# The second product of a feed-forward layer computed with seven half-size products instead of eight

## The chip, the cores and the metric

The kernel runs on one core of a Trainium2 chip. The metric is the device time in microseconds, the median of several runs. All data is fp32 unless a line says otherwise. Engines are called PE (TensorE), DVE (VectorE), ACT (ScalarE), POOL (GpSimd) and SP (SyncE, which issues nearly all DMAs).

## The reference, cut to what matters

The input has four batches of 2048 tokens of 256 features. It is normalized, and two branches run on the normalized `xn`: a linear-attention layer with its feed-forward part, and a gated feed-forward with 4-bit block quantization. Their product is added to the input.

```python
def _L0_attn_ref(src, Wq, bq, ...):
    q = (src @ Wq + bq).reshape(b, s, H, DH)      # k, v alike; H = 16, DH = 64
    Q = elu(q) + 1.0
    K = elu(k) + 1.0
    KV = einsum('bshd,bshm->bhdm', K, v)
    Z = 1.0 / (einsum('bshd,bhd->bsh', Q, K.sum(axis=1)) + EPS)
    o = einsum('bshd,bhdm,bsh->bshm', Q, KV, Z).reshape(b, s, H * DH)
    x = layer_norm(src + o @ Wo + bo, g1, be1)
    y = gelu(x @ W1 + b1) @ W2 + b2               # W1 256 x 1024, W2 1024 x 256
    return layer_norm(x + y, g2, be2)

def _L0_ffn_ref(x, w_gate, w_up, w_down):
    h = silu(fp4_linear(x, w_gate)) * fp4_linear(x, w_up)
    return fp4_linear(h, w_down)                  # quantized in blocks of 16

xn = layernorm(x)
s = _L0_attn_ref(xn, ...)
g = silu(_L0_ffn_ref(xn, ...))
out = x + s * g
```

The change concerns one product, `gelu(...) @ W2`.

## The kernel before

The 8192 tokens are worked in 32 blocks of 256 tokens (`NBLK` = 32, eight blocks a batch, `NB` = 8). A block is two tiles of 128 tokens, because a tile has 128 partitions. Attention needs the key sums of a whole batch before its first query, so blocks 0 to 23 also carry the keys of the batch after theirs (`keys_k`, `keys_xk`, two tiles, "subs", a block), and blocks 24 to 31 have no key work. The keys of batch 0 are made in a prologue, during which the weights are loaded one after the other (`later`, L182 to L193; a tiny POOL copy in `load_when` holds each load back until some `kk` is there).

The main loop (L967 to L1074) issues, for block n, in this order on PE:

1. `q_of(n)`: the query product `pq`, its exponential on ACT, `zq` on DVE;
2. the keys of the first sub: product `pk`; on DVE the add of the bias `k1` (L471); the exponential `ek` on ACT; the combination `kk` on DVE (L480); the product `pxk` of `kk` with `xn_k`;
3. `sums(n)` (L747): `pz`, on DVE `z = 1/pz`, which goes to memory and comes back spread over the partitions as `zb` (four DMAs);
4. `gate_up(n+1)` and `down(n)`: the quantized branch, products `pg` and `pd`. After `pd`, ACT makes `g` and three POOL operations of 128x512 (L713 to L715) follow as a burst;
5. `qz(n)` (L774): two DVE multiplications of 128x1024, `zq *= zb`;
6. the keys of the second sub (`pk`, `k1`, `kk` as in 2);
7. `attention(n)` (L780): 16 matmuls `pa` of `zq` with the folded matrix `m`; on DVE the sum `x1 = xn + pa` and its normalization;
8. `pxk` of the second sub;
9. `ffn_2(n-1)`: the product `py` = `hT` x `w2_sb` for the block before, split: 12 of its 16 matmuls here (in blocks without keys four stand before `attention` and eight here);
10. `x1_T(n)`: transposes `pt_x` of x1, then `spread_scales(n+1)`: a transpose `pscale` of the quantization scales, which go to memory and come back spread in eight DMAs as `qT`, which `pd` of the next block reads; between and after them the last four matmuls of `py`;
11. `output(n-1)` (L842): on DVE `s = x1 + py`, the statistics, two scalings, and the store;
12. `ffn_1(n)` (L811): the product `pf`, and on ACT the GELU that writes `hT`, the transposed hidden layer (8 chunks of 128 hidden features by 256 tokens).

An fp32 `mm` of the code is two MATMUL instructions on PE. PE's order is exactly that of the program:

```python
    def mm(*args, **kw):
        return tc.keep_in_program_order(nc.tensor.matmul(*args, **kw))
```

The other engines keep program order in the prologue only. In the main loop a scheduler at build time sets the order of the operations of DVE, ACT, POOL and SP, unless `tc.issue_after(x)` puts an operation behind x. All DVE and ACT operations are recorded by a helper at L115, so the profile names that line for all of them.

Buffers: `ps` has four PSUM banks that rotate under the tag "mm" (`mm_tile`), `pacc` has two "acc" banks for `pa` and `py` (`acc_tile`) and two for `pxk`. In SBUF a tag is a set of slots that tiles take in turn: `zb` has one slot, `s` one, `kv` one, `ksum` one, `x1` two, `kk` three, `big` (with `hT`) two. A tile that takes a slot waits for the last reader of the tile before it.

The second product before, for token tile j:

```python
    def ffn_2(n, j, chunks=range(NF)):
        ...
        for c in chunks:
            mm(
                py[:, j, :], hT[:, c, j * P : (j + 1) * P], w2_sb[:, c, :],
                start=c == 0, stop=c == NF - 1,
            )
```

With NF = 8 chunks and two tiles that is 16 matmuls of N=256, 32 instructions.

Of the kernel before, what the change touches and what calls it, by code (L numbers as in the profile page):

```python
# [8 lines left out]
F32 = mybir.dt.float32  # L9
# [3 lines left out]
ALU = mybir.AluOpType  # L13
AX = mybir.AxisListType

P = 128
# [6 lines left out]
def linear_attention_gated_by_fp4_ffn(  # L23
# [34 lines left out]
    nc = tc.nc  # L58
    B, S, D = src.shape
# [6 lines left out]
    NF = FF // P  # L66
# [21 lines left out]
    def acc_tile(name, tag="acc"):  # L88
        return pacc.tile([P, 512], F32, tag=tag, name=name)

    def rows_of(dst, n):

        b, bi = divmod(n, NB)
        return dst[b, bi * T : (bi + 1) * T, :].rearrange("(p j) d -> p j d", j=TB)
# [34 lines left out]
    def load_when(dep, t, v, eng=nc.sync):  # L129

        if dep is not None:
            first = t[:1, 0, :1] if len(t.shape) == 3 else t[:1, :1]
            nc.gpsimd.tensor_copy(first, dep[:1, :1])
        eng.dma_start(t, v)
# [30 lines left out]

    wq_sb = const.tile([P, ND, HD], F32, name="wq_sb")
    w1_sb = const.tile([P, ND, FF], F32, name="w1_sb")
    w2_sb = const.tile([P, NF, D], F32, name="w2_sb")
    row_tiles = {
        name: const.tile([P, 1, D], F32, name=f"{name}_r")  # L170
        for name in ("bo", "g1", "shift", "g2", "be2")
# [3 lines left out]
    def by_chunks(w):  # L175
        return w.rearrange("(c p) f -> p c f", p=P)

    def load_row(name, v, dep):
        load_when(dep, row_tiles[name][:, 0, :], as_rows(v))


    later = {  # L182
        0: [lambda dep: load_row("bo", bo, dep)],
# [5 lines left out]
            lambda dep: load_row("g2", g2, dep),  # L189
            lambda dep: load_row("be2", be2, dep),  # L190
        ],
        5: [lambda dep: load_when(dep, w2_sb, by_chunks(W2))],
    }  # L193

    cols = {}
# [265 lines left out]
    def key_product(xnT, f, j, nm):  # L461

        fs = slice(f * HALF, (f + 1) * HALF)
        pk = mm_tile(f"pk_{nm}_{j}")
        for c in range(ND):
            mm(
                pk, xnT[:, c, j * P : (j + 1) * P], wk_sb[:, c, fs],
                start=c == 0, stop=c == ND - 1,
            )
        k1 = work.tile([P, HALF], F32, tag="q1", name=f"k1_{nm}_{j}", bufs=3)  # L470
        vector.tensor_tensor(k1, pk, bk1[:, fs], ALU.add)  # L471
        e = work.tile([P, HALF], F32, tag="e", name=f"ek_{nm}_{j}", bufs=3)
        keys["exp"] = scalar.activation(e, k1, AF.Exp, bias=neg_one).ins
        return k1, e
# [40 lines left out]
    def m_of_half(b, f, dep=None, ahead=False):  # L515


        nm = f"{b}_{f}"
        fs = slice(f * HALF, (f + 1) * HALF)
        wv = batch.tile([P, ND, HALF], F32, tag="wv", name=f"wv_{nm}", bufs=1)  # L520
        load_when(dep, wv, by_chunks(Wv)[:, :, fs])
        wo = batch.tile([P, 4, D], F32, tag="wo", name=f"wo_{nm}", bufs=1)
        load_when(dep, wo, by_chunks(Wo)[:, 4 * f : 4 * f + 4, :])
        if ahead:
            yield
        if f == 0:
            kh[b] = batch.tile([P, NH, 32], F32, tag="kh", name=f"kh_{b}")
            nc.gpsimd.memset(kh[b], 0.0)
        m = m_sb[b, f] = batch.tile([P, 4, D], F32, tag="m", name=f"m_{nm}", bufs=3)
        kacc = keys.pop((b, "acc", f))  # L530
        pxk = keys.pop((b, "pxk", f))
        xk = batch.tile([P, ND, HALF], F32, tag="xk", name=f"xk_{nm}", bufs=1)
        for d in range(ND):
            scalar.copy(xk[:, d, :], pxk[d])

        pks = mm_tile(f"pks_{nm}")
        mm(pks[:1, :], ones[:, 0:1], kacc, start=True, stop=True)
        krow = work.tile([P, HALF], F32, tag="x1T", name=f"krow_{nm}", bufs=1)[:1, :]
        scalar.copy(krow, pks[:1, :])
        k_d = dram.tile([1, HALF], F32, tag="k_d", name=f"k_d_{nm}", bufs=2)  # L540
        nc.sync.dma_start(k_d, krow)
        yield
        ksum = work.tile([P, 4, P], F32, tag="ksum", name=f"ksum_{nm}", bufs=1)
        nc.sync.dma_start(
            ksum, k_d.rearrange("o (c f) -> o c f", c=4).to_broadcast([P, 4, P])
        )

        own = work.tile([P, 4, P], F32, tag="kv", name=f"own_{nm}", bufs=1)
        kcol = small.tile([P, 4], F32, tag="kcol", name=f"kcol_{nm}")
        vector.tensor_tensor(own, ksum, ident.unsqueeze(1).to_broadcast([P, 4, P]), ALU.mult)  # L550
        vector.tensor_reduce(kcol, own, AX.X, ALU.add)
        for i in range(2):
            hs = slice(i * DH, (i + 1) * DH)
            r0 = 2 * f + i
            vector.tensor_copy(kh[b][hs, 4 * f : 4 * f + 4, r0], kcol[hs, :])
        yield

        pkv = mm_tile(f"pkv_{nm}")[:, : 4 * DH].rearrange("p (c f) -> p c f", c=4)
        kv = work.tile([P, 4, P], F32, tag="kv", name=f"kv_{nm}", bufs=1)
        nc.gpsimd.memset(kv, 0.0)  # L560
        for ci in range(4):
            for d in range(ND):
                for h in range(2):
                    cs = slice(ci * P + h * DH, ci * P + (h + 1) * DH)
                    mm(
                        pkv[h * DH : (h + 1) * DH, ci, :], wv[:, d, cs], xk[:, d, cs],
                        start=d == 0, stop=d == ND - 1,
                    )
        for ci in range(4):
            for h in range(2):  # L570
                hs = slice(h * DH, (h + 1) * DH)
                c = 4 * f + ci
                vector.scalar_tensor_tensor(
                    kv[hs, ci, hs], ksum[hs, ci, hs], cols["bv"][hs, c : c + 1],
                    pkv[hs, ci, :], ALU.mult, ALU.add,
                )
        yield
        for c2 in range(2):
            pm = mm_tile(f"pm_{nm}_{c2}").rearrange("p (c d) -> p c d", c=2)
            for ci in range(2):  # L580
                mm(
                    pm[:, ci, :], kv[:, 2 * c2 + ci, :], wo[:, 2 * c2 + ci, :],
                    start=True, stop=True,
                )
            scalar.copy(m[:, 2 * c2 : 2 * c2 + 2, :], pm)
        yield
# [187 lines left out]
    def qz(n):  # L774
        zq, zb = blk[n]["zq"], blk[n].pop("zb")
        for g in range(2):
            cs = slice(4 * g, 4 * g + 4)
            vector.tensor_tensor(zq[:, cs, :], zq[:, cs, :], zb[:, cs, :], ALU.mult)
# [50 lines left out]
                )  # L829
        blk[n]["gelu"] = ins.ins  # L830

    def ffn_2(n, j, chunks=range(NF)):
        if "py" not in blk[n]:
            blk[n]["py"] = acc_tile(f"py_{n}").rearrange("p (j d) -> p j d", j=TB)
        py, hT = blk[n]["py"], blk[n]["hT"]
        for c in chunks:
            mm(
                py[:, j, :], hT[:, c, j * P : (j + 1) * P], w2_sb[:, c, :],
                start=c == 0, stop=c == NF - 1,
            )  # L840

    def output(n, js=range(TB)):  # L842
        j0, j1 = js[0], js[-1] + 1
        g, o, x1, py = (blk[n][k] for k in ("g", "o", "x1", "py"))
        s = work.tile([P, TB, D], F32, tag="s", name=f"s_{n}_{j0}", bufs=1)
        vector.tensor_tensor(s[:, j0:j1, :], x1[:, j0:j1, :], py[:, j0:j1, :], ALU.add)
        mv, rstd = stats(s, f"2_{n}_{j0}", js)
        for j in js:
            vector.scalar_tensor_tensor(
                s[:, j, :], s[:, j, :], mv[:, j, 0:1], g[:, j, :], ALU.subtract, ALU.mult  # L850
            )
        for j in js:
            vector.scalar_tensor_tensor(
                o[:, j, :], s[:, j, :], rstd[:, j : j + 1], o[:, j, :], ALU.mult, ALU.add
            )
        nc.sync.dma_start(rows_of(out, n)[:, j0:j1, :], o[:, j0:j1, :])


    def step(gen, times=1):
        for _ in range(times):  # L860
            next(gen, None)
# [94 lines left out]
        keys_in(1, sub)  # L956
    spread_scales(0, True, True)
    step(down_1)
    for j in range(TB):
        grid_of_h(0, j)  # L960
    grid_of_x(1)
# [5 lines left out]
    for n in range(NBLK):  # L967
# [43 lines left out]
                down(n, j)  # L1011
        with tc.issue_after(blk[n + 1]["late"]) if n < last else nullcontext():
            qz(n)
        if subs:
            keys_k(b + 1, subs[1])
        elif n > 0:
            ffn_2(n - 1, 0, range(NF // 2))
        attention(n)
        if n + 2 < NBLK:
            load_xn(n + 2)  # L1020
# [7 lines left out]
        for sub in next_subs if n > 0 else ():  # L1028
            keys_in(bn + 1, sub)
        if n > 0:  # L1030
            ffn_2(n - 1, 0, range(0 if subs else NF // 2, NF))
            ffn_2(n - 1, 1, range(NF // 2))
        more = n + 1 < NBLK, n + 2 < NBLK
        if more[0]:
            for j in range(TB):
# [8 lines left out]
        for sub in next_subs[1:]:  # L1044
            keys_apart(bn + 1, sub, blk[n]["act"])

        half_way = NF // 2 if subs else 3 * NF // 4
        if n > 0:
            ffn_2(n - 1, 1, range(NF // 2, half_way))
        if more[0]:  # L1050
            spread_scales(n + 1, *more)
        if n > 0:
            ffn_2(n - 1, 1, range(half_way, NF))
        if more[0]:
            grid_of_h(n + 1, 0)
            grid_T(n + 1, 0, NI)
# [12 lines left out]
            ffn_1(n)  # L1069
        for sub in next_subs[:1]:  # L1070
            keys_T(bn + 1, sub, blk[n]["gelu"])
    for j in range(TB):
        ffn_2(last, j)
        output(last, [j])  # L1074


# [32 lines left out]
```

## Time and profile before

| | |
|---|---|
| median of three runs | 1934.9 us (1933.09 to 1935.98) |
| the profiled execution | 1931.66 us |
| its span, first to last instruction | 1929.9 us |
| mean granted PE clock | 0.999 |
| PE busy in 0 to 140 us (prologue) | 131.51 us |
| PE busy in 204 to 1140 us | 934.31 of 936 us |
| PE busy in 1140 to 1580 us | 440.00 of 440 us |
| PE busy in 1580 to 1872 us (blocks without keys) | 291.61 of 292 us |
| PE busy in 1872 to 1930 us (the end) | 50.51 of 58 us |
| `py` matmuls: busy in all, mean of one | 234.4 us, 380 ns |
| DVE waits for `ek` before `kk` | 50.2 us in all, 72 times |
| DVE waits for ACT before `zq` | 123.1 us in all, 72 times |

Times that follow are counted from the first instruction of the span. A row of the timeline has the start, the duration from the first start to the last end of the instructions that the row joins, the engine, the line, the operation, the tiles written and read, the tile sizes, the number of instructions and, in brackets, how long the engine stood idle before and what ended that. The mean duration of a matmul (380 ns) is longer than the distance between two starts, because matmuls are pipelined. What one costs the engine is the distance between starts.

### The profile page before, as it was taken

Reading aid. Unit: us, or ns where it says so; the run is one execution under the profiler, and the core shown is the slowest. Engines: PE = TensorE matmul, PEld = TensorE weight load, DVE = VectorE, ACT = ScalarE, POOL = GpSimd, SP = SyncE. Lnnn points to the kernel's source line nnn. Section 1 sums busy time; section 2 is a strip of 40 time slices with the busy share of each in tenths; the row PEclk is TensorE's granted clock in tenths of the full one; section 3 lists DMA queues with packets and bytes.
Section 4 is the critical chain, followed back from the end, with each engine's and each line's share of the span. In section 5 each row is a group of like instructions: output and inputs, shape, how many; then the busy total and the mean of one; then the engine's idle time right before and its main releaser. Section 6 shows DMA issues by size and latency. Waiting matters only on the chain.

```text
span 1929.9 us, 22642 instructions
## 1 busy us (share of the span) xinstructions
PE 1906.7 (99%) x8020; PEld 1369.5 (71%) x8020; DVE 1270.7 (66%) x2300; ACT 802.9 (42%) x1384; POOL 534.5 (28%) x455
## 2 busy tenths in 40 slices
PE   9999999999999999999999999999999999999998
PEld 4446677667777677777677776677776777777787
DVE  7878666666566666666666666666565676677763
ACT  2334454334444355542344543454433443334442
POOL 4431232322233222322222323222232212222212
PEclk9999999999999999999999999999999999999999
DMA  4425545344434455543443554464433444444442
GB/s 153 147 93 121 111 103 113 99 107 85 93 63 94 116 100 115 127 92 96 91 87 71 114 105 102 96 124 94 100 80 73 76 81 86 81 86 82 86 85 48
DMA packets 224184, 186.99 MB, mean 97 GB/s; under 512 B 103332, under 2 KB 184768, under 8 KB 224072
## 3 DMA queue, kind: packets, MB, share of 16 engines
q1 hardware_dynamic: 223240, 183.99, 44.9%
q10 hardware_dynamic: 832, 1.57, 0.3%
q8 instruction: 63, 1.03, 0.2%
q14 instruction: 49, 0.40, 0.1%
HBM read 131.41 MB, written 31.54 MB: 84 GB/s over the span
## 4 chain that ended last, share of the span: by engine, by line
PE 84%; DMA 2%; DVE 1%; ACT 1%; SPq 1%; issue 0%; POOL 0%; POOLq 0%; DVEq 0%; ACTq 0%
PE pg L99 15%; PE py L99 11%; PE pa L99 11%; PE pf L99 10%; PE pq L99 10%; PE pxk L99 8%; PE pk L99 8%; PE pd L99 8%; PE pz L99 2%; DMA qT<-scale_d 1%; PE pt_x L102 1%; PE pm L99 1%; SPq L648 0%; DVE zq L115 0%; DMA zb<-z_d 0%
## 5 line engine op out<-in xcount | busy, mean ns | idle before, releaser
L99 PE MATMUL pg<-wgu,qT 128*128 128x352 f32 x1024 | 310.4, 461 | 0.0
L99 PEld LDWEIGHTS pg<-wgu,qT 128*128 128x128 f32 x1024 | 193.2, 190 | 118.6 <-issue 13.9
L484 POOL TENSOR_TENSOR kacc<-kacc,kk 128x512 f32<-128x512 f32 x120 | 171.2, 1427 | 304.8 <-DVE kk L115 302.7
L99 PE MATMUL pxk<-kk,xn_k 128*128 128x512 f32 x512 | 235.9, 599 | 3.4 <-DVE kk L115 3.3
L99 PE MATMUL py<-w_sb,hT 128*128 128x256 f32 x1024 | 234.4, 380 | 0.5 <-DVE s L115 0.5
L99 PE MATMUL pk<-wk_sb,xnT_k 128*128 128x512 f32 x512 | 230.4, 593 | 2.2 <-ACT xnT_k L115 1.8
L99 PE MATMUL pq<-xnT,wq_sb 128*128 128x256 f32 x1024 | 227.4, 380 | 1.6 <-ACT hT L115 1.6
L99 PE MATMUL pa<-m,zq 128*128 128x256 f32 x1024 | 227.3, 380 | 1.6 <-DVE zq L115 1.6
L99 PE MATMUL pf<-x1T,w_sb 128*128 128x256 f32 x1024 | 226.6, 379 | 0.0
L99 PEld LDWEIGHTS pa<-m,zq 128*128 128x128 f32 x1024 | 193.9, 190 | 40.1 <-issue 11.3
L99 PEld LDWEIGHTS py<-w_sb,hT 128*128 128x128 f32 x1024 | 191.0, 190 | 38.0 <-issue 8.1
L99 PEld LDWEIGHTS pq<-xnT,wq_sb 128*128 128x128 f32 x1024 | 195.2, 191 | 28.7 <-ACT hT L115 2.0
L99 PEld LDWEIGHTS pf<-x1T,w_sb 128*128 128x128 f32 x1024 | 194.3, 190 | 27.0 <-ACT hT L115 0.4
L713 POOL TENSOR_TENSOR o<-g,be_r 128x512 f32<-128x512 f32 x32 | 48.6, 1518 | 579.2 <-ACT g L115 579.2
L115 ACT ACT_TABLE_LOAD x122 | 156.5, 1283 | 96.1 <-DVE k L115 82.4
L99 PE MATMUL pd<-wd,qT 128*128 128x256 f32 x768 | 172.4, 379 | 0.1
L99 PEld LDWEIGHTS pk<-wk_sb,xnT_k 128*128 128x128 f32 x512 | 97.0, 190 | 103.8 <-issue 96.8
L99 PEld LDWEIGHTS pxk<-kk,xn_k 128*128 128x128 f32 x512 | 92.5, 190 | 109.3 <-issue 80.6
L115 DVE SCALAR_TENSOR_TENSOR zq<-e,q 128x512 f32<-128x512 f32 x128 | 86.9, 688 | 123.2 <-ACT e L115 123.1
L99 PEld LDWEIGHTS pd<-wd,qT 128*128 128x128 f32 x768 | 145.6, 190 | 24.8 <-DVE qT L115 1.3
L359 POOL TENSOR_TENSOR rstd<-rstd,neg_half 128x2 f32<-128x2 f32 (+1 forms) x97 | 72.8, 751 | 303.2 <-DVE rstd L115 259.5
L115 ACT ACTIVATE x1T<-pt_x,bcol 128x256 f32<-128x256 f32 x64 | 32.6, 560 | 257.6 <-PE pt_x L102 257.6
(123 smaller groups left out, 2337.6 us busy)
## 6 DMA issues: line engine op xcount, KB each, us to landing
zb<-z_d SPq DMA_DIRECT2D x128, 256.0 KB, 5.6
qT<-scale_d SPq DMA_DIRECT2D x248, 128.0 KB, 5.7
x_k<-in_L_attn_src_dram SPq DMA_DIRECT2D x32, 256.0 KB, 3.2
x<-in_L_attn_src_dram SPq DMA_DIRECT2D x32, 256.0 KB
xn_d<-xn_k SPq DMA_DIRECT2D x32, 256.0 KB, 3.5
xn<-xn_d SPq DMA_DIRECT2D x32, 256.0 KB, 2.5
xnT_d<-xnT_k SPq DMA_DIRECT2D x32, 256.0 KB, 4.2
xnT<-xnT_d SPq DMA_DIRECT2D x32, 256.0 KB, 2.7
```

What stands on the lines that cost most here:

```text
L99: return tc.keep_in_program_order(nc.tensor.matmul(*args, **kw))
L102: return tc.keep_in_program_order(nc.tensor.transpose(*args, **kw))
L115: ins = op(*args, **kw)
L359: nc.gpsimd.tensor_tensor(rstd[:, j0:j1], rstd[:, j0:j1], neg_half[:, j0:j1], ALU.pow)
L484: nc.gpsimd.tensor_tensor(kacc, kacc, kk, ALU.add)
L713: nc.gpsimd.tensor_tensor(o, g, rows["be2"], ALU.mult)
```

## The change

The product of a block is Y = H x W2, H being 256 tokens by 1024 hidden features and W2 1024 by 256. Each is cut in halves both ways: H into h11, h12, h21, h22 (first index the token tile, second the half of the hidden features, four chunks), W2 into four quarters of 512 by 128. Strassen's algorithm in Winograd's form needs seven products of halves instead of eight, with sums of halves on both sides:

- sums of h, four DVE operations of 128x512 a block, both inputs in SBUF: s3 = h11 - h21, s1 = h21 + h22, s2 = s1 - h11, s4 = h12 - s2;
- sums of W2, once, on POOL, in place of the quarters that only appear in sums;
- the quarters of Y are sums of the seven products, added straight to `x1` in `output`.

Each product has four chunks, so a block has 28 matmuls of N=128 (56 instructions) instead of 16 of N=256 (32 instructions). The seven products fill two PSUM banks: py0 holds products 2, 3, 4, 1, and py1 holds 6, 7, 5. One of the two comes from the "mm" banks and the other from "acc", and which one depends on n.

The sums of h stand in the one slot of the tag `zb`, so they can only be written when `qz` of the same loop turn has read its `zb`, and the next `zb` can only be loaded when the products have read the sums.

Core of the diff:

```diff
-    w2_sb = const.tile([P, NF, D], F32, name="w2_sb")
+    NF2 = NF // 2
+    w2_sb = const.tile([P, 7, NF2, P], F32, name="w2_sb")
+    W2_OF = {"11": 0, "21": 1, "22": 2, "t1": 3, "t2": 4, "t3": 5, "t4": 6}
...
+    def load_w2(dep):
+        for q, i, j in (("11", 0, 0), ("t1", 0, 1), ("21", 1, 0), ("22", 1, 1)):
+            load_when(
+                dep, w2(q), by_chunks(W2)[:, i * NF2 : (i + 1) * NF2, j * P : (j + 1) * P]
+            )
+
+    def w2_sums():
+        nc.gpsimd.tensor_tensor(w2("t3"), w2("22"), w2("t1"), ALU.subtract)
+        nc.gpsimd.tensor_tensor(w2("t1"), w2("t1"), w2("11"), ALU.subtract)
+        nc.gpsimd.tensor_tensor(w2("t2"), w2("22"), w2("t1"), ALU.subtract)
+        nc.gpsimd.tensor_tensor(w2("t4"), w2("21"), w2("t2"), ALU.subtract)
...
-        5: [lambda dep: load_when(dep, w2_sb, by_chunks(W2))],
+        5: [lambda dep: load_w2(dep)],
...
-        vector.tensor_tensor(k1, pk, bk1[:, fs], ALU.add)
+        with tc.issue_after(keys["kh"]) if "kh" in keys else nullcontext():
+            vector.tensor_tensor(k1, pk, bk1[:, fs], ALU.add)
...
-        ksum = work.tile([P, 4, P], F32, tag="ksum", name=f"ksum_{nm}", bufs=1)
+        ksum = work.tile([P, 4, P], F32, tag="x1", name=f"ksum_{nm}")
...
-        own = work.tile([P, 4, P], F32, tag="kv", name=f"own_{nm}", bufs=1)
+        own = work.tile([P, 4, P], F32, tag="kk", name=f"own_{nm}", bufs=3)
...
-        kv = work.tile([P, 4, P], F32, tag="kv", name=f"kv_{nm}", bufs=1)
+        kv = work.tile([P, 4, P], F32, tag="s", name=f"kv_{nm}", bufs=1)
...
+    def ffn_sums(n):
...
+        t = work.tile([P, 4, NF2, P], F32, tag="zb", name=f"hs_{n}", bufs=1)
+        s1, s2, s3, s4 = (t[:, i] for i in range(4))
+        vector.tensor_tensor(s3, h["11"], h["21"], ALU.subtract)
+        vector.tensor_tensor(s1, h["21"], h["22"], ALU.add)
+        vector.tensor_tensor(s2, s1, h["11"], ALU.subtract)
+        vector.tensor_tensor(s4, h["12"], s2, ALU.subtract)
+        blk[n]["ffn"] = {
+            1: (h["11"], "11"), 2: (h["12"], "21"), 3: (s4, "22"), 4: (h["22"], "t4"),
+            5: (s1, "t1"), 6: (s2, "t2"), 7: (s3, "t3"),
+        }
+
+    PY_SLOT = {2: (0, 0), 3: (0, 1), 4: (0, 2), 1: (0, 3), 6: (1, 0), 7: (1, 1), 5: (1, 2)}
+
+    def ffn_2(n, to, order=(1, 2, 4, 3, 5, 7, 6)):
...
+        for at in range(done, to):
+            i, c = order[at // NF2], at % NF2
+            bank, slot = PY_SLOT[i]
+            if bank not in py:
+
+                t = (mm_tile if (bank == 0) == (n >= NBLK - NB - 1) else acc_tile)(f"py{bank}_{n}")
...
             mm(
-                py[:, j, :], hT[:, c, j * P : (j + 1) * P], w2_sb[:, c, :],
-                start=c == 0, stop=c == NF - 1,
-            )
+                py[bank][:, slot, :], h[:, c, :], w2(w)[:, c, :], start=c == 0, stop=c == NF2 - 1
+            )
...
-        vector.tensor_tensor(s[:, j0:j1, :], x1[:, j0:j1, :], py[:, j0:j1, :], ALU.add)
+        vector.tensor_tensor(s4, x4, py[0], ALU.add)
+        vector.tensor_tensor(s4[:, :3, :], s4[:, :3, :], of(0, 3, 3), ALU.add)
+        vector.tensor_tensor(s4[:, 1:, :], s4[:, 1:, :], of(1, 0, 3), ALU.add)
+        vector.tensor_tensor(s4[:, 2:, :], s4[:, 2:, :], of(1, 1, 2), ALU.add)
+        vector.tensor_tensor(s4[:, 1::2, :], s4[:, 1::2, :], of(1, 2, 2), ALU.add)
...
             qz(n)
+        if not subs:
+            ffn_2(n - 1, 4 if n < last else 8)
+        if n > 0:
+            ffn_sums(n - 1)
         if subs:
             keys_k(b + 1, subs[1])
-        elif n > 0:
-            ffn_2(n - 1, 0, range(NF // 2))
         attention(n)
...
         if n > 0:
-            ffn_2(n - 1, 0, range(0 if subs else NF // 2, NF))
-            ffn_2(n - 1, 1, range(NF // 2))
+            ffn_2(n - 1, 20)
...
-        half_way = NF // 2 if subs else 3 * NF // 4
-        if n > 0:
-            ffn_2(n - 1, 1, range(NF // 2, half_way))
+        if n > 0 and not subs:
+            ffn_2(n - 1, 26)
         if more[0]:
             spread_scales(n + 1, *more)
         if n > 0:
-            ffn_2(n - 1, 1, range(half_way, NF))
+            ffn_2(n - 1, 28)
...
-    for j in range(TB):
-        ffn_2(last, j)
-        output(last, [j])
+    ffn_2(last, 4)
+    ffn_sums(last)
+    ffn_2(last, 28, (1, 7, 2, 4, 5, 3, 6))
+    output(last)
```

`ffn_2(n, to)` now issues the matmuls of the seven products in the given order up to the number `to` of 28. In blocks with keys 20 stand before `x1_T` and 8 after `spread_scales`; in blocks without keys 4 stand before `attention`, 16 after it, 6 after `x1_T` and 2 after `spread_scales`. The output of the last block, which was made in two halves, each with a store of its own, is now made whole.

More of the change, by code (lines that the diff above doesn't have):

```diff
@@ L179, in load_row, with w2 @@
         load_when(dep, row_tiles[name][:, 0, :], as_rows(v))
+    def w2(q):
+        return w2_sb[:, W2_OF[q]]
+    def load_w2(dep):
[8 more added lines that the diff above has]
+        nc.gpsimd.tensor_tensor(w2("t4"), w2("21"), w2("t2"), ALU.subtract)
     later = {
@@ L554, in m_of_half @@
             r0 = 2 * f + i
-            vector.tensor_copy(kh[b][hs, 4 * f : 4 * f + 4, r0], kcol[hs, :])
+            ins = vector.tensor_copy(kh[b][hs, 4 * f : 4 * f + 4, r0], kcol[hs, :])
+            if f > 0:
+                keys["kh"] = ins.ins
         yield
         pkv = mm_tile(f"pkv_{nm}")[:, : 4 * DH].rearrange("p (c f) -> p c f", c=4)
-        kv = work.tile([P, 4, P], F32, tag="kv", name=f"kv_{nm}", bufs=1)
+        kv = work.tile([P, 4, P], F32, tag="s", name=f"kv_{nm}", bufs=1)
         nc.gpsimd.memset(kv, 0.0)
@@ L830, in ffn_1 @@
         blk[n]["gelu"] = ins.ins
[L832 to L836, printed above, removed]
-            mm(
-                py[:, j, :], hT[:, c, j * P : (j + 1) * P], w2_sb[:, c, :],
-                start=c == 0, stop=c == NF - 1,
-            )
-    def output(n, js=range(TB)):
-        j0, j1 = js[0], js[-1] + 1
+    def ffn_sums(n):
+        hT = blk[n]["hT"]
+        h = {
+            f"{i + 1}{k + 1}": hT[:, k * NF2 : (k + 1) * NF2, i * P : (i + 1) * P]
+            for i in range(2) for k in range(2)
+        }
[8 more added lines that the diff above has]
+            5: (s1, "t1"), 6: (s2, "t2"), 7: (s3, "t3"),
+        }
@@ new lines, in linear_attention_gated_by_fp4_ffn @@
+    PY_SLOT = {2: (0, 0), 3: (0, 1), 4: (0, 2), 1: (0, 3), 6: (1, 0), 7: (1, 1), 5: (1, 2)}
+    def ffn_2(n, to, order=(1, 2, 4, 3, 5, 7, 6)):
+        py = blk[n].setdefault("py", {})
+        done = blk[n].get("done", 0)
+        blk[n]["done"] = to
+        for at in range(done, to):
[3 more added lines that the diff above has]
+                t = (mm_tile if (bank == 0) == (n >= NBLK - NB - 1) else acc_tile)(f"py{bank}_{n}")
+                py[bank] = t.rearrange("p (s d) -> p s d", s=4)
+            if "ffn" in blk[n]:
+                h, w = blk[n]["ffn"][i]
+            else:
+                hT = blk[n]["hT"]
+                h, w = {
+                    1: (hT[:, :NF2, :P], "11"), 2: (hT[:, NF2:, :P], "21"),
+                    4: (hT[:, NF2:, P:], "t4"),
+                }[i]
+            mm(
+                py[bank][:, slot, :], h[:, c, :], w2(w)[:, c, :], start=c == 0, stop=c == NF2 - 1
+            )
@@ L844, in output, with quarters, of @@
+    def output(n):
         g, o, x1, py = (blk[n][k] for k in ("g", "o", "x1", "py"))
-        s = work.tile([P, TB, D], F32, tag="s", name=f"s_{n}_{j0}", bufs=1)
-        vector.tensor_tensor(s[:, j0:j1, :], x1[:, j0:j1, :], py[:, j0:j1, :], ALU.add)
-        mv, rstd = stats(s, f"2_{n}_{j0}", js)
-        for j in js:
+        s = work.tile([P, TB, D], F32, tag="s", name=f"s_{n}", bufs=1)
+        def quarters(t):
+            return t.rearrange("p j (h d) -> p (j h) d", h=2)
+        def of(bank, slot, n):
+            return py[bank][:, slot : slot + 1, :].to_broadcast([P, n, P])
+        s4, x4 = quarters(s), quarters(x1)
+        vector.tensor_tensor(s4, x4, py[0], ALU.add)
[3 more added lines that the diff above has]
+        vector.tensor_tensor(s4[:, 1::2, :], s4[:, 1::2, :], of(1, 2, 2), ALU.add)
+        mv, rstd = stats(s, f"2_{n}")
+        for j in range(TB):
@@ L851, in output @@
             )
-        for j in js:
+        for j in range(TB):
             vector.scalar_tensor_tensor(
@@ L855, in output @@
             )
-        nc.sync.dma_start(rows_of(out, n)[:, j0:j1, :], o[:, j0:j1, :])
+        nc.sync.dma_start(rows_of(out, n), o)
     def step(gen, times=1):
@@ L958, in linear_attention_gated_by_fp4_ffn @@
     step(down_1)
+    w2_sums()
     for j in range(TB):
```

## The prediction

> **What bounds the kernel now.** I read the busy totals first, then the forty slices, the windows by stage, the timeline of one block in each stage, and last the waits of TensorE.
>
> ```profile
> PE 1906.7 (99%) x8020; PEld 1369.5 (71%) x8020; DVE 1270.7 (66%) x2300; ACT 802.9 (42%) x1384; POOL 534.5 (28%) x455
> PE   9999999999999999999999999999999999999998
> 905.00:1140.00 235.00, 235.00 (x991) 169.68 (x990) 147.41 (x274) 97.56 (x167) 63.94 (x53) 1.00 0.43 89
> ```
>
> The third line is a window over four blocks of the main loop (sum, then PE, PEld, DVE, ACT, POOL busy, clock, DMA): TensorE never pauses. TensorE's order is written by hand, so a matmul less is worth its time, and anything that makes TensorE wait is lost in full. The waits of TensorE are small now, 3.3 us in all for `kk`. How near the next wait is, a block's timeline shows; block 13, TensorE:
>
> ```profile
> 951.25 7.07 PE L99 MATMUL pa<-m,zq 128*128 128x256 f32 x32
> 958.16 3.60 PE L99 MATMUL pxk<-kk,xn_k 128*128 128x512 f32 x8
> 961.59 5.34 PE L99 MATMUL py<-w_sb,hT 128*128 128x256 f32 x24
> 966.77 0.60 PE L102 MATMUL pt_x<-ident,x 128*128 128x128 f32 x4
> 967.21 0.27 PE L102 MATMUL pscale<-ident,scale 128*128 128x128 f32 x1
> ```
>
> VectorE and GpSimd ahead of the `kk` that `pxk` needs:
>
> ```profile
> 946.33 1.22 DVE L115 TENSOR_TENSOR zq<-zq,zb 128x1024 f32<-128x1024 f32 x1
> 947.46 0.88 DVE L115 TENSOR_REDUCE scale<-h 128x44 f32<-128x704 f32 x1
> 948.26 0.88 DVE L115 SCALAR_TENSOR_TENSOR grid<-m_h,h 128x704 bf16<-128x704 bf16 x1
> 949.06 1.25 DVE L115 TENSOR_SCALAR scale<-scale 128x44 f32<-128x44 f32 x1
> 950.81 1.56 DVE L115 SCALAR_TENSOR_TENSOR h<-h,rs_h 128x704 f32<-128x704 f32 x1
> 952.28 1.28 DVE L115 TENSOR_TENSOR k<-pk,bk 128x512 f32<-128x512 f32 x2
> 955.09 1.38 DVE L115 SCALAR_TENSOR_TENSOR kk<-ek,k 128x512 f32<-128x512 f32 x2 [1.53 <-ACT ek L115]
> ```
> ```profile
> 948.75 1.51 POOL L713 TENSOR_TENSOR o<-g,be_r 128x512 f32<-128x512 f32 x1 [15.75 <-ACT g L115]
> 950.35 1.27 POOL L714 TENSOR_TENSOR o<-o,x 128x512 f32<-128x512 f32 x1
> 951.57 1.93 POOL L715 TENSOR_TENSOR g<-g,g_r 128x512 f32<-128x512 f32 x1
> ```
>
> To be seen: VectorE has no gap from 946.33 to 953.5; the first `kk` is ready at 955.09 + 0.69 = 955.8, 2.4 us before `pxk` starts. And the two engines alternate: the small TENSOR_SCALAR takes 1.25 us beside a GpSimd operation (the like of it took 0.18 alone), and GpSimd's 1.27 us becomes 1.51 and 1.93.
>
> **What the Trainium skill says.** "SBUF — State Buffer", section on who interferes with whom: a VectorE instruction with two SBUF inputs contends with a GpSimd instruction that reads SBUF, and the second to issue is blocked. The lines above agree. "VectorE: DVE Perf Modes": an fp32 tensor_tensor stays at one element a cycle; the 128x512 `x<-xn,pa` at 0.69 us fits. "TensorE: Matmul & The Clock Gate", section LDWEIGHTS: a load takes time by its columns, about 107 ns for 128, and can bind at small N. The trace shows 190 ns for a 128-column load, started under the matmul before, and 81 for one column, so about 109 ns of it grow with the columns.
>
> **The change, part by part.**
>
> 1. *Products.* A fp32 matmul is two instructions. Removed: 32 instructions of N=256 a block at 5.18 us / 24 = 216 ns (start of `py` to start of `pt_x`): 6.91 us. Added: 7 x 4 x 2 = 56 of N=128. The trace has 128-wide fp32 transposes at 0.44 / 4 = 110 ns, and 109 ns is also what a load needs: 56 x 0.109 = 6.10 us. So -0.81 us a block, -25.9 in 32 blocks. Bounds: the pace can't be under half of 216 (108); if load and stream don't overlap fully, 125 to 130 ns, which makes 7.0 to 7.3 us and no gain. I take 109.
>
> 2. *Sums of h, blocks 1 to 23.* Four VectorE operations of 128x512 with both inputs in SBUF, 0.61 us each back to back (0.69 less overlap): 2.45 us. Because they sit in the slot of `zb`, they must follow `qz`; the build puts them after the second `qz`, between the scales and the rounding of `h`, ahead of the `k` adds. So all of it falls on the chain `k`, `ek`, `kk`, `pxk`. They also fall on GpSimd's burst. Worked through block 13 by alternation: reduce to 948.3, s3 to 948.9, GpSimd to 950.1, s1 to 950.75, GpSimd to 951.95, scale to 952.1, GpSimd to 953.3, then grid, s2, reciprocal, s4 and `h` to 956.6. First `k` add 4.3 us later than 952.28; it ends `kk` 3.5 us on, at 960.1, and `pxk` stands from 958.16: 2.0 us lost. I did so for all 23 blocks, from the end of `qz` and the start of the burst in each. The distance from first `kk` to `pxk` is, for n = 1 to 23: 4.5 4.6 2.0 2.0 0.9 2.2 2.4 4.9 4.8 3.9 0.7 0.4 2.4 2.2 4.3 4.9 4.8 4.4 2.4 4.0 2.1 2.6 4.6 us. Result: 3 to 7, 11 to 14, 19, 21, 22 lose about 2.1 each (25.7); 1, 2, 10, 15, 18, 20, 23 together 8.5; where `zb` comes long before the burst (8, 9, 16, 17) nothing. Together 34 us. Lower bound: no blocking, 2.45 us against the distances: 7.4 us. I take 34, since blocking shows in the lines above both ways. What is queued behind: `k` adds, then ScalarE's exponentials and GpSimd's `kacc`; nobody waits for `kacc` soon. The stall delays the `x1` chain no more than TensorE itself.
>
> 3. *Output, same blocks.* One 512-wide add becomes five (512, 384, 384, 256, 256, one input in PSUM: some 0.69, 0.55, 0.55, 0.42, 0.42), 1.9 us more. Hidden: VectorE is idle until the `zq` of the next block (123 us in all, behind `e`). The bank of py1 is then free 1.7 us before the next `pq` needs it. Nothing; uncovered it would cost the part over 1.7.
>    1 to 23 together: -0.81 x 23 = -18.6, +34: +15.4. Block 24: -0.3.
>
> 4. *Blocks 25 to 30* (no keys). Half of `pa` already waits for `qz`:
>
> ```profile
> 1680.60 7.31 PE L99 MATMUL pa<-m,zq 128*128 128x256 f32 x32
> 1687.75 3.62 PE L99 MATMUL py<-w_sb,hT 128*128 128x256 f32 x16
> 1692.69 0.27 PE L102 MATMUL pscale<-ident,scale 128*128 128x128 f32 x1
> ```
> ```profile
> 1680.91 1.50 DVE L115 TENSOR_TENSOR zq<-zq,zb 128x1024 f32<-128x1024 f32 x1
> 1687.95 0.69 DVE L115 TENSOR_TENSOR x<-xn,pa 128x512 f32<-128x512 f32 x1 [2.44 <-PE pa L99]
> 1692.06 0.18 DVE L115 TENSOR_SCALAR scale<-scale 128x32 f32<-128x32 f32 x1
> ```
>
>    `zq` ends at 1682.4, the ninth of `pa` starts at 1680.60 + 8 x 0.216 = 1682.3. The 0.87 us that eight N=128 instructions save ahead of `pa` turn into a wait. Behind it the sums push the `x1` add by 0.5 us (s4 is ahead of it), and two `s` adds from py0 (1.2 us) stand before the scale: it is ready at 1692.24 + 1.7 = 1693.9, 1.25 us after `pscale` runs now. From `pscale` the scales go through memory to `qT`, 13.7 us, and `pd` had 0 to 0.17 us to spare: +1.25 a block, 7.5 for six. Lower bound +0.4 for all, if the adds slip behind the scale. I take 7.5.
>
> 5. *Block 31 and the end.* +0.3. At the end the products save 0.8, and the 0.5 us in which `py` waits for `s` goes; but the last product is followed by three adds (0.55 + 0.42 + 0.42) instead of one of 0.42, by statistics and scaling of both halves (about +1.35 by rows of 0.43, 0.18, 0.47, 0.48 us, part of it overlapped) and a store of double size (0.5, between 0 and 1): +1.5.
>
> 6. *Prologue.* W2 in four loads on SyncE's queue, and four GpSimd sums (4 x 1.27 = 5.1 us) that wait for the last of them and stand before `kacc` and an `rstd` at 102.1 us: that goes to about 106. Key blocks behind it have most of this covered: +1.5, between 0 and 4. The moves of `ksum`, `own`, `kv` into other slots and the later `k1` add in blocks with `kh` copies: nothing, at most 0.5.
>
> Sum: +15.4 - 0.3 + 7.5 + 0.3 + 1.5 + 1.5 = +25.9. Span 1929.9 + 25.9 = 1955.8, with the 1.8 us around it 1957.6; the median of runs is 3.2 us over the profiled execution: **1961**.
>
> **Rivals.**
> A. As above. Its own range: half of the blocking, and the lower bound in part 4, give about 1945; 0.15 us more a block and the prologue at 4 give 1976.
> B. *Not slower: the sums miss the burst.* Place: VectorE between the second `qz` and the first `k` add. If those adds come at most the distance (mean 3.1 us) later, `pxk` does not wait and the saving lives: -18.6 + 7.4 - 0.3 + 2.7 + 1.5 + 1 = -6, 1929; with no stall at all 1922. It decides from a delay of about 2.5 us down. For it: in four blocks `zb` comes long before the burst. Against: two GpSimd operations hit VectorE in the block shown even without the sums.
> C. *Even.* Stalls of 0.6 to 0.8 us a block eat the saving exactly: 1931 to 1939.
> D. *The load binds at N=128.* At 122 to 130 ns the products cost what they did or more, and A's stalls come on top, partly filled: +26 + 14 to 38, 1975 to 2000. For it: 190 ns for one load, twice as many loads per column. Against: the transposes hold 110 ns.
>
> **How the numbers follow.** A 0.63, B 0.22, C 0.06, D 0.09. A measurement of this kernel can tell 0.2%, 3.9 us, from no change. Low 1926 (B's likely part), high 1976 (A's top); beyond lie D and the tail of B. Faster 0.23, same 0.06, slower 0.71.
>
> **What would show it.** Right: TensorE waits for `kk` 25 to 40 us in all (3.3 now), in the middle of blocks; `py` at 109 ns; `pd` waiting for `qT` in 25 to 30; `pscale` waits up. Wrong: `kk` waits under 10 us, or `py` above 120 ns, or the time to the first `k` add grown by less than 2.5 us.

## The result and the profile after

The changed kernel takes 1947.68 us (median of four runs, 1943.76 to 1948.53) where the kernel before takes 1934.27: ratio 1.0065, 95% interval 1.0047 to 1.0082. It is slower by about 13 us. The forecast was 1961, slower by 26: the sign came true, the size was twice what was measured. The profiled execution took 1948.53 us, its span 1946.4, which is 16.5 us more than before. The two profiled executions lie some 3 us further apart than the medians: that of before is 2.6 us under its median, that of the changed kernel 0.9 over.

The busy totals of the page after the change, and TensorE's largest waits (time in all, number of waits, longest):

```profile
PE 1895.5 (97%) x8788; PEld 1379.9 (71%) x8788; DVE 1440.9 (74%) x2554; ACT 803.7 (41%) x1384; POOL 562.3 (29%) x461
```

Before:

```profile
PE pxk L99 <- DVE kk L115: 3.3, 3, 1.8
```

After:

```profile
PE pxk L99 <- DVE kk L115: 19.6, 14, 1.9
PE pa L99 <- DVE zq L115: 8.0, 7, 2.8
```

TensorE is busy for 11.2 us less (1906.7 before), and the span is 16.5 longer: TensorE now waits. The wait that was forecast is there, `pxk` for `kk`, 19.6 us where it was 3.3; `pa` for `zq` grew from 1.6 to 8.0. `pscale` waits as before, in the prologue and block 0 only.

Block 13 again, after the change. VectorE:

```profile
952.00 1.22 DVE L115 TENSOR_TENSOR zq<-zq,zb 128x1024 f32<-128x1024 f32 x1
...
953.93 1.28 DVE L115 TENSOR_TENSOR hs<-hT 128x512 f32<-128x512 f32 x2
955.13 1.25 DVE L115 TENSOR_SCALAR scale<-scale 128x44 f32<-128x44 f32 x1
956.30 0.88 DVE L115 SCALAR_TENSOR_TENSOR grid<-m_h,h 128x704 bf16<-128x704 bf16 x1
957.10 1.75 DVE L115 TENSOR_TENSOR hs<-hs,hT 128x512 f32<-128x512 f32 x1
...
959.12 1.42 DVE L115 TENSOR_TENSOR hs<-hT,hs 128x512 f32<-128x512 f32 x1
960.46 0.88 DVE L115 SCALAR_TENSOR_TENSOR h<-h,rs_h 128x704 f32<-128x704 f32 x1
961.26 1.27 DVE L115 TENSOR_TENSOR k<-pk,bk 128x512 f32<-128x512 f32 x2
```

GpSimd's burst, and TensorE:

```profile
954.55 1.79 POOL L735 TENSOR_TENSOR o<-g,be_r 128x512 f32<-128x512 f32 x1 [15.75 <-ACT g L115]
956.42 1.89 POOL L736 TENSOR_TENSOR o<-o,x 128x512 f32<-128x512 f32 x1
958.27 1.72 POOL L737 TENSOR_TENSOR g<-g,g_r 128x512 f32<-128x512 f32 x1
```
```profile
957.05 7.07 PE L99 MATMUL pa<-m,zq 128*128 128x256 f32 x32
964.81 3.70 PE L99 MATMUL pxk<-kk,xn_k 128*128 128x512 f32 x8 [0.69 <-DVE kk L115]
```

From the second `qz` (start 952.00) to the first `k` add are 9.26 us, where it was 952.28 - 946.33 = 5.95: 3.3 us later, not 4.3. `pa` has 32 instructions of 216 ns, so TensorE was ready at 957.05 + 6.91 = 963.96, and `pxk` started 0.85 us after that. The forecast for this block was 2.0.

Where the 16.5 us came from shows when the start of each block's first `pq` is set against that of before. All rows in us of the span:

| part | forecast | measured |
|---|---|---|
| prologue and block 0 | +1.5 | +3.9 |
| blocks 1 to 23 | +15.4 | +2.3 |
| block 24 | -0.3 | +1.5 |
| blocks 25 to 30 | +7.5 | +5.7 |
| block 31 and the end | +1.8 | +3.1 |

The 23 blocks divide sharply. Eleven (1, 2, 7 to 10, 15 to 18, 23) take 0.66 us less than before each. The other twelve (3 to 6, 11 to 14, 19 to 22) lose between 0.14 and 1.9 us at `pxk`, 16.1 in all, and a little behind it: 23 x 0.66 = 15.2 gained, 17.4 lost.

A rival is the clock. From 6 us on TensorE has the full clock in the changed kernel's trace, except in four stretches at half of it: 3.41 us from 8.97, 6.83 from 152.33, 3.41 from 1828.28, and the last 5.5 us, behind the last matmul. Before there are two: 3.41 us from 151.28, and the last 0.2 us. An estimate from the clock of 0.50 is that half the time in which TensorE is busy there is lost: 6.1 us after, 1.7 before. So some 4 of the 16.5 us lie there, in the prologue, block 0 and block 29. Blocks 1 to 23 have the full clock in both traces, and what they lose is no matter of the clock.

### The profile page after: what moved, and what is told of

Its sections match the earlier page's. It is cut to its first block, busy times and chain, and to the rows that moved or that the text cites. A ratio compares the mean times of both kernels' runs of the same rounds, so it can differ in the third digit from the quotient of the medians.

```text
span 1946.4 us, 24467 instructions
## 1 busy us (share of the span) xinstructions
PE 1895.5 (97%) x8788; PEld 1379.9 (71%) x8788; DVE 1440.9 (74%) x2554; ACT 803.7 (41%) x1384; POOL 562.3 (29%) x461
## 5 line engine op out<-in xcount | busy, mean ns | idle before, releaser
L99 PE MATMUL pxk<-kk,xn_k 128*128 128x512 f32 x512 | 237.1, 602 | 19.7 <-DVE kk L115 19.6
L377 POOL TENSOR_TENSOR rstd<-rstd,neg_half 128x2 f32<-128x2 f32 x96 | 72.8, 759 | 283.4 <-DVE rstd L115 266.2
L115 ACT ACTIVATE h<-pg 128x352 f32<-128x352 f32 x128 | 58.9, 460 | 191.5 <-PE pg L99 191.5
L115 ACT ACTIVATE ek<-k,neg_one 128x512 f32<-128x512 f32 x128 | 89.7, 719 | 116.3 <-DVE k L115 115.9
L115 DVE SCALAR_TENSOR_TENSOR kk<-ek,k 128x512 f32<-128x512 f32 x128 | 90.2, 713 | 61.6 <-ACT ek L115 61.6
```

The lines of the kernel that those rows point to most:

```text
L115: ins = op(*args, **kw)
L377: nc.gpsimd.tensor_tensor(rstd[:, j0:j1], rstd[:, j0:j1], neg_half[:, j0:j1], ALU.pow)
```

## The experiments

Two theories stood against each other. Theory A: the sums of h on VectorE, together with GpSimd's burst, delay the `k` adds, and `pxk` waits. Theory C: it is not the sums, but a later `zb` or the narrower matmuls. Within A it was open what decides, the 2.45 us of the sums or their collisions with the burst. All variants start from the changed kernel.

**The sums of h left out (`e1_no_h_sums`).** The products take plain quarters of `hT` instead.

```diff
-        s1, s2, s3, s4 = (t[:, i] for i in range(4))
-        vector.tensor_tensor(s3, h["11"], h["21"], ALU.subtract)
...
+        s1, s2, s3, s4 = h["21"], h["22"], h["11"], h["12"]
```

> The four sums of h are left out; the products take plain quarters of hT in their place, so the products, the output adds and the order of TensorE stay. Theory A (the sums on VectorE, with what GpSimd's burst adds, make pxk wait for kk): the 12 blocks that lost 17.4 us lose nothing, each block with keys takes about 0.66 us less than before, and the span falls from 1946.4 to about 1929, or to 1925 if blocks 25 to 30 gain as well. Theory C (the loss comes from zb arriving later or from the narrower matmuls, not from the sums): the same blocks still wait, span above 1940.

Measured: 1923.54 us, 0.995 of before (0.9935 to 0.9965), span 1920.3. Every block from 1 to 23 took 0.64 to 0.66 us less than before; together -15.1. So the narrower matmuls make nothing wait, and their saving stands: 6.91 - 0.66 = 6.25 us for 56 instructions, 112 ns each. The span is even below the expected 1925, because the prologue, block 24, blocks 25 to 30 and the end also cost 9 us less than in the changed kernel. The slot of `zb` is freed here too, so this run alone doesn't exclude a later `zb`. The traces do: in the twelve late blocks the second `qz` ends on average 30.46 us after the first `pq` of the block before the change and 30.35 after it. So C falls.

**The sums behind the second `kk` (`e2_sums_behind_kk`).**

```diff
         if subs:
-            keys_k(b + 1, subs[1])
+            kk_ins = keys_k(b + 1, subs[1])
+            if n > 0:
+                with tc.issue_after(kk_ins):
+                    ffn_sums(n - 1)
```

> The sums are queued behind the second kk of the block instead of ahead of the k adds, in blocks with keys only. Theory A: the waits of pxk for kk go from 19.6 to about 3 us, the blocks take 57.1 us again, and the span falls by about 17 to 1929. The x1 chain gets at most 2.5 us later and has 2.8 us to spare. Rival (VectorE is too full there wherever the sums stand): pt_x or pscale waits instead, and the span stays above 1938.

Measured: 1927.88 us, 0.9976 of before (0.9965 to 0.9987): faster than both kernels. VectorE in block 13 of this variant:

```profile
950.04 1.28 DVE L115 TENSOR_TENSOR k<-pk,bk 128x512 f32<-128x512 f32 x2
...
954.14 3.43 DVE L115 TENSOR_TENSOR hs<-hT 128x512 f32<-128x512 f32 x2
...
958.95 0.68 DVE L115 TENSOR_TENSOR x<-xn,pa 128x512 f32<-128x512 f32 x1
```

The `k` adds start 5.95 us after the start of the second `qz` (944.09), as before the change, and no `pxk` of blocks 1 to 23 waits, although the sums still stand in the slot of `zb`. The first two sums now collide with GpSimd's `kacc` instead (3.43 us for two that take 1.28 without), but that lies in front of the `x1` add, which had room. The rival has a small part: blocks 4, 5, 6 and 12 lose the saving again, and `pscale` waits 1.7 us more in all than before. Blocks 1 to 23 came to -11.9, 3.2 us short of `e1`.

**The burst later (`e3_burst_late`).**

```diff
-        nc.gpsimd.tensor_tensor(o, g, rows["be2"], ALU.mult)
...
+        ins = nc.gpsimd.tensor_tensor(x1, x1, rows["shift"], ALU.add)
+        with tc.issue_after(ins.ins):
+            burst(n)
```

> The sums stay where the change put them; GpSimd's burst of three operations after pd is queued behind its two operations on x1, some 15 us later. If the collisions decide: the k adds come 2.5 to 3 us earlier, kk is ready in time in nearly all blocks, waits of pxk under 5 us, span about 1931. If the 2.45 us of the sums alone decide: the blocks with less than 2.5 us to spare go on waiting, waits of pxk 12 us or more, span above 1940.

Measured: 1992.88 us, 1.0305 of before (1.029 to 1.032). No `pxk` of blocks 1 to 23 waits any longer, as A with deciding collisions expects, yet the kernel is 45 us slower still. The burst had found new victims. GpSimd, VectorE and TensorE at the end of block 13:

```profile
990.37 1.93 POOL L739 TENSOR_TENSOR o<-g,be_r 128x512 f32<-128x512 f32 x1
...
993.94 1.92 POOL L741 TENSOR_TENSOR g<-g,g_r 128x512 f32<-128x512 f32 x1
```
```profile
992.77 1.96 DVE L115 SCALAR_TENSOR_TENSOR grid<-m_h,h 128x704 bf16<-128x704 bf16 x1
994.65 1.83 DVE L115 SCALAR_TENSOR_TENSOR grid<-m_x,y 128x256 bf16<-128x256 bf16 x2
996.40 1.45 DVE L115 TENSOR_TENSOR s<-s,py 128x384 f32<-128x384 f32 x3
```
```profile
997.96 2.40 PE L99 MATMUL pq<-xnT,wq_sb 128*128 128x256 f32 x10 [1.44 <-issue]
```

Each rounding waits for a GpSimd operation (0.88 for a `grid` in the block above, 1.96 here), the last reads of py1 end at 997.85, and the next `pq`, which takes that bank, starts at 997.96 after 1.44 us of standing. That is the cover of part 3 of the prediction gone. Such waits of `pq` make up most of what blocks 1 to 23 lose, 23 us more than in the changed kernel. Another 23 us are lost in blocks 24 to 30, where `pd` waits 2.4 to 3.5 us in every block, nearly always for `qT`, and where TensorE has half its clock in six stretches, 27.3 us in all, beside six of these seven waits. The place of the burst is no free choice; so a test without the burst was needed.

**No burst (`e7_no_burst`).** `be2`, `g2` and the added input are left out.

> The changed kernel with GpSimd's burst after pd left out (the factors be2 and g2 and the added x are left out, o is taken straight from x), the order on VectorE nearly unchanged. If the collisions with the burst decide whether pxk waits: as in e3, the waits of pxk are under 5 us, without e3's waits of pq, and the span is about 1929. If e3's other waits came from the sums, pq waits here too. If the four sums alone are too much, pxk still waits 7 us or more in all.

Measured, in one run: 1922.65 us, span 1920.8. `pxk` waits 5.6 us in all, 0.34 of it in blocks 1 to 23; these blocks came to -14.4. VectorE in block 13 has the sums where the change put them:

```profile
947.10 1.28 DVE L115 TENSOR_TENSOR hs<-hT 128x512 f32<-128x512 f32 x2
948.30 0.18 DVE L115 TENSOR_SCALAR scale<-scale 128x44 f32<-128x44 f32 x1
...
949.20 0.68 DVE L115 TENSOR_TENSOR hs<-hs,hT 128x512 f32<-128x512 f32 x1
...
950.14 0.62 DVE L115 TENSOR_TENSOR hs<-hT,hs 128x512 f32<-128x512 f32 x1
...
951.48 1.28 DVE L115 TENSOR_TENSOR k<-pk,bk 128x512 f32<-128x512 f32 x2
```

The same scale operation takes 0.18 instead of 1.25, the third and fourth sum 0.68 and 0.62 instead of 1.75 and 1.42. That is the exclusive blocking which the Trainium skill describes ("SBUF — State Buffer", who interferes with whom), seen here with the same operation in the same place. In the twelve late blocks the way from the end of the second `qz` to the first `k` add is 4.74 us on average before, 8.12 after, 5.09 with the burst late and 4.89 without it. The burst therefore costs 3.0 to 3.2 us of the 8.12, and sums without burst take hardly longer than burst without sums. The sums alone make TensorE wait 0.34 us in blocks 1 to 23, in block 13; sums and burst together make it wait 16.1. The margin without the burst is thin, though: in blocks 5 and 14 `kk` is ready 0.06 us before `pxk` starts.

**Seven products only where there are keys (`e5_keys_only`).** On top of `e2`; from block 24 on the eight products of before, with the output of the end in halves, and the overwritten quarter of W2 loaded again.

```diff
+        if n == NBLK - NB:
+            nc.sync.dma_start(w2("t1"), by_chunks(W2)[:, :NF2, P:])
...
+        elif n > 0:
+            ffn_2_plain(n - 1, 0, range(NF // 2, NF))
+            ffn_2_plain(n - 1, 1, range(NF // 2))
...
+    for j in range(TB):
+        ffn_2_plain(last, j)
+        output_plain(last, [j])
```

> Seven products only where the block in hand has keys (blocks 1 to 23, sums behind the second kk); from block 24 on the eight products of before, with their output in halves at the end; the quarter of W2 that the sums overwrote is loaded again for it. If seven products cost as much as they save in blocks 24 to 31, and the whole output costs 3 us at the end, the span falls from 1925.0 to about 1920 (1929.9 less 23 times 0.66, plus some 5 for the prologue and block 0 and single waits); the last block's output again ends about 5.3 us after the last matmul instead of 8.4. If seven products pay in blocks 24 to 31 as well, it stays at 1925 or rises.

Measured: 1925.95 us, 0.9965 of before (0.9952 to 0.9977), span 1923.4, not the 1920 expected. Blocks 25 to 30 cost +1.0 against the kernel before, though they have the same eight products (+0.6 in `e6`), where `e2` had +3.3 and the changed kernel +5.7: seven products cost some 2 us there beside the burst. Without the burst (`e7`) they came to -0.8 in these blocks, so there too the burst has a part. At the end the last store is issued 2.7 us after the last matmul as before, not 5.4 as in the changed kernel.

But block 24 gave back 2.1, 1.33 of it where `pd` starts late, and block 31 with the end 1.6, where `pa` stands 1.4 us longer for `zq`. Both stand in the trace of `e6` as well, whose code is the same there (block 24 +2.4; `pa` of block 31 waits 2.8 us in each), so they look like a property of this variant. Which transfer or queue makes them was not tried. The intervals of `e2` and `e5` overlap, so which of the two is better is open; both beat the kernel before.

**The sums of W2 elsewhere (`e4_w2_sums_in_block0`, `e6_w2_sums_at_150`).** In `e4` they are queued behind GpSimd's work on the x1 of block 0, in `e6` (on top of `e5`) behind its addition of `bo` near 150 us.

```diff
-    w2_sums()
...
+            with tc.issue_after(blk[0]["x1s"]):
+                w2_sums()
```
```diff
-    w2_sums()
...
+    with tc.issue_after(grid_of_x(1)):
+        w2_sums()
```

> The four GpSimd sums of W2 move from the prologue behind GpSimd's work on x1 of block 0. If they are what delays the prologue, the first pq comes 2 to 3 us earlier than in the changed kernel (it was 3.2 us later than before); if the four loads or chance in the first loads do it, it stays within 1 us of there. The sums of h are unchanged, so the total falls by that amount only.

> As e5, with the four GpSimd sums of W2 held back until GpSimd has added bo to the xn of block 1, near 150 us, where GpSimd stands idle for 17 us. If the sums of W2 cost the prologue 2.5 us by holding up an rstd and by collisions with the kk of VectorE, the span falls by about 2.4 below that of e5; if it is chance, it stays within 0.5 of it.

Measured: `e4`, in one run, 1944.9 us, within the range of the changed kernel's four runs; the prologue came to +1.3 instead of +3.3, and block 0 to +3.6 instead of +0.7, with a wait of 5.4 us of `pq` for `hT`. `e6` took 1926.31 us, 0.9966 of before (0.9955 to 0.9977), the same as `e5`. In its trace both waits of `pxk` near 103 and 112 us are as in the kernel before, and a later start of `pscale` (+1.3 us) took their place. In `e4` too these waits are as before, while the three waits of `pxk` from 103 to 125 us grew from 3.3 to 5.4 us in all in the changed kernel. So the sums of W2 do delay the prologue by some 2 us where the change puts them, and neither of two other places was seen to be worth anything in the time.

## Why the prediction was half right

The verdict "slower", the place (`pxk` for `kk` in blocks with keys) and the mechanism (sums and burst block each other) came true. The step that failed is the size in part 2: "First `k` add 4.3 us later", and from it 34 us of waiting. Measured: 3.4 us later on average over the twelve late blocks (8.12 - 4.74), and 16.1 us of waiting.

- *Delay by collisions.* In block 13 the forecast was 2.45 us for the sums and 1.85 for blocking on top of what was there before: each of GpSimd's three operations was to hold VectorE for its whole length, 3.6 us, where the lines of before show 1.75 (1.07 at the scale, 0.68 at `h`). Set against the same operations without the burst (`e7`), the lines of after show 2.94: 1.07 at the scale, 1.07 and 0.80 at the third and fourth sum. So the blocking grew by 1.2 us, and the other 2.1 of the 3.3 are the sums. GpSimd bore a part of the waiting: its first operation met the second sum and took 1.79 us instead of 1.27, and the rounding `grid` came ahead of GpSimd's second operation and was not held (0.88).
- *Blocks with an early `zb`.* The 8.5 us of waiting for seven of them, and the 2 us for block 7, came to 0.14, in block 20. In nine of the eleven blocks that lost nothing the first `k` add had stood 1.92 us after the start of `pk`; it went to at most 5.5, and the 3.6 us were less than the distances of 4.3 to 4.9 us. In block 7 `zb` came 1.4 us earlier than in the execution that I had worked from.
- *Lower bound.* The 7.4 us "no blocking" left the collisions of before in place. No run has the sums with those alone; without the burst they go too, and the waits are 0.34 us.
- *Products.* 0.81 us a block was forecast, 0.66 measured: 112 ns for N=128, not 109. Rival D is out.
- *Output in blocks with keys.* Hidden, as forecast; `e3` shows waits of `pq` where the adds come later.
- *Blocks 25 to 30.* +5.7 for +7.5, but not by the way described. The profile of block 26:

```profile
1689.83 5.45 PE L99 MATMUL pa<-m,zq 128*128 128x256 f32 x24 [0.56 <-DVE zq L115]
...
1699.29 1.50 PE L99 MATMUL py<-w_sb,hs 128*128 128x128 f32 x12
1700.90 0.33 PE L102 MATMUL pscale<-ident,scale 128*128 128x128 f32 x1
```

  `pa` waits for the second `zq`, as forecast. But `pscale` comes 0.73 us later against `pt_x`, not 1.25 against its old place: most of that is its place in TensorE's order, behind 12 narrow matmuls instead of four wide ones, and the `x1` add was hardly late (1695.42, `pa` ending at 1695.28). And `pd` waited for `qT` in two of the six blocks only (0.6 us in block 26, 1.1 in block 30). Blocks 25 to 28 cost +0.4 in all; 3.3 of the 5.7 is block 29, and 2.1 block 30. Block 29, the same 24 matmuls of `pa`, and the window at half clock (the 0.50, third from the end):

```profile
1826.86 7.13 PE L99 MATMUL pa<-m,zq 128*128 128x256 f32 x24 [2.42 <-DVE zq L115]
1828.28:1831.69 3.41, 3.41 (x10) 2.69 (x9) 3.18 (x6) 0.00 (x0) 0.00 (x0) 0.50 0.00 1
```

  A late `zb`, and a rounding that the burst held (1.98 us instead of 0.88), make `pa` wait 2.42 us. The half clock then takes 1.7 us more (7.13 against 5.45 in block 26). Less the 0.8 us that eight narrow matmuls save ahead of `pa`, that is the 3.3. In `e2`, with the same code there, block 29 was 0.5 us shorter than before and block 30 2.6 longer. So at least block 29's loss is no fixed price.
- *The end.* +3.1 for block 31 and the end, where +1.8 was forecast. The last store was issued 5.4 us after the last matmul instead of 2.7: all five adds, statistics and scalings of both halves stand there. I priced the statistics and scalings at 1.35 us less overlap, beside the adds. In block 31 `pa` also waited 2.75 us for `zq`, 1.2 more than before.
- *Prologue.* +3.9 with block 0 where 1.5 was taken, within the bounds of 0 and 4. The `rstd` went to 105.1 us (forecast: about 106), and the waits of `pxk` behind it grew by 2.1. The rest is the clock. 0.9 was there at the first `pxk`, behind the stretch at half clock near 9 us: twelve matmuls `pk` take 7.11 us across it, and 5.42 in `e1`, which has no such stretch; that is 1.7 us, less 0.7 by which `pk` began earlier than before. Only `e4` and `e7` have that stretch too, and only these start that `pxk` as late. The other 0.9 is the stretch at 152 us, twice as long as before.

With 16.1 in place of 34 the forecast span would have been 1937.9, 8.5 us below the measured 1946.4. The other terms were too low by that much: 3.5 for the products and 1.3 behind `pxk` in blocks 1 to 23, 3.8 for the other stages together. So the forecast total came closer than its main term by luck, two errors of opposite sign.

## What to carry to other kernels

When work is added beside a burst of another engine, a whole operation of the burst for each collision is too much to charge: the other engine does some of the waiting, and an operation is held only for what is left of the one before it (here 2.94 us of blocking where 3.6 was charged). Fewer multiplications help a full TensorE only if the sums that they need stand where its next input does not queue behind them: against no sums at all, the same four sums cost blocks 1 to 23 17.3 us ahead of the `k` adds and 3.2 behind `kk`. A different place for the blocking engine's work is a change of its own, which can be worse. And before a loss in a trace is explained by a queue, the clock of that stretch is to be looked at: two of the losses here were in part half clock.

## What the runs showed of the hardware

- fp32 matmuls of N=128, each with a weight load of its own, ran at 112 ns against 216 for N=256, so a half-width product costs only 3 to 4% more than half.
- A tiny VectorE operation can pay the most: the 128x44 scale took 0.18 us without the burst and 1.25 beside it, while the `k` adds with one input in PSUM took 1.27 to 1.28 for two in the blocks shown, also beside a GpSimd operation (952.28 before the change, with GpSimd busy from 951.57 to 953.50).
- Three GpSimd operations a block in the wrong place cost 45 us over the run (`e3` against the changed kernel), over three times what the change itself had cost. By the estimate above, some 13 us of that are lost at half clock.
- A wait of TensorE can cost more than itself. A stretch of 3.41 us at half clock stands behind the 2.42 us wait of block 29, and stretches of 3.41 or 6.83 us beside six of the seven `pd` waits in blocks 24 to 30 of `e3`. It does not always follow: behind the wait of 2.81 us of `pa` in block 31 such a stretch came in `e6` and none in `e5`. What decides it these runs don't show.
